# Neighbouring states of a selective scan added in pairs on GpSimd before TensorE sums them, in batch 3 of 4

## The chip, the core and the metric

The kernel runs on one core of a Trainium2 chip. The metric is the device time of one execution in microseconds (us). In the kernel before, three runs gave 2015.58, 2021.76 and 2025.78 us; their median is 2021.76 us. Engines are called PE (TensorE; PEld is its weight load), DVE (VectorE), ACT (ScalarE), POOL (GpSimd) and SP (SyncE, which here issues the DMAs).

## The reference, cut to what matters

Two layers run on x (4 batches of 512 tokens of 512 features) with a context (4 of 512 x 256): a selective state-space block gated by x, a ternary feed-forward block ("bitnet"), a cross attention with 16 heads, and four small experts. The change lies in the first block:

```python
def step(state, xs):
    d_t, B_t, C_t, u_t = xs
    dA = jnp.exp(d_t[..., None] * A)
    state = state * dA + (d_t * u_t)[..., None] * B_t[:, None, :]
    y_t = jnp.einsum('ben,bn->be', state, C_t)
    return (state, y_t)
...
y = y + D[None, :, None] * u
y = y * jax.nn.silu(z)
```

There are 512 channels, 512 steps in time and 16 states. The sum over the 16 states n in `y_t` is what the change regroups.

## The kernel before

Each batch goes through `front` (projections, L524), `scan` (L606), `bitnet` (L710) and `attention` (L826, 16 heads). Batch 0 does the first three alone. From batch 1 on, those three of batch b run beside the attention heads of batch b-1: the main loop (L1301) takes a piece of a head, then some steps of `layer0` (L1284), which is front, scan and bitnet of a later batch (`LEADS` says from which head). Batch 3's scan so runs beside the last heads of batch 1 and the first of batch 2. Below, "head 1.14" is batch 1's head 14. The order on each engine is then not that of the text: a scheduler places the instructions, and each engine works through its own list strictly in that order.

The scan takes the 512 channels as four tiles of 128 and works on two of them (t = 0, 1) at a time: a first half (t0 = 0) and a second (t0 = 2). In a half, for each state n and tile t:

- ACT makes dA = exp(delta A) in PSUM (L652);
- POOL multiplies u by B into a tile h (L656, by the helper at L186; it shows as h<-u,bc);
- DVE scans along time (L659 or L662);
- the product with C is made by DVE (L660) in six of eight steps, and by POOL (L663, by L186; it shows as h<-h,cc) in the other two, which fall on odd n and t = 1;
- PE adds the product into the accumulator `py` by four 128x128 transposes (`add`, L625, at L627), which accumulate in PSUM over all 16 states; `uds`, the D u term, is added the same way after n = 2 (L665).

B and C of each state are broadcast to all partitions by two DMAs (bc, L646; cc, L648) into tiles of tag "g", of which there are five. The tiles h have the tag "v", of which there are six (`MIDS`, L67). After a half, `silu_z` (L610) of the batch's x is used (first half) or read back (second half) for the gate, and the sum is added to x (L683). Batch 3's x takes the buffer of batch 1's x, so `load_x(3)` (L640, by L179) waits until batch 1 has left it (`finish`, L1273). `silu_z` then needs four `row_stats` (L188), whose reciprocal roots are on POOL (L183, rstz).

A head makes queries (pq) and their norms on POOL (rqs, L942), scores (ps), a softmax in two halves (L954) and the weighted sum (pav). In the heads from 9 on of batches 0 to 2, POOL makes one column of each softmax half (L984 and L986, `LO_POOL`), otherwise it makes only a scaled copy (L991). After four heads there is a projection (pwo). POOL also makes parts of the keys (rk, L874; ks, L889).

Of the kernel before, what the change touches and what calls it, by code (L numbers as in the profile page):

```python
# [35 lines left out]
ALU = mybir.AluOpType  # L36
# [10 lines left out]
DS = 16  # L47
# [44 lines left out]
SC = 4  # L92
PT = 3
MT = 0
AV = 4
VB = 2
WB = 5
# [13 lines left out]
def flamingo_kernel(  # L111
# [8 lines left out]
    nc = tc.nc  # L120
# [11 lines left out]
    def psum(pool, name, tag="m", bufs=None):  # L132
        if tag == "a":
            role = name.rstrip("_0123456789")
            if pool is psa and role in LAST_PSS and name[len(role)] == str(B - 1):
                return psum(pss, name)
            tag = ATAG.get(role, "m")
            bufs = ABUF[tag]
        kw = {} if bufs is None else {"bufs": bufs}
        return pool.tile([P, 512], F32, tag=tag, name=name, **kw)  # L140
# [12 lines left out]
    def midt(shape, dtype, name, tag):  # L153
        if tag in wider:
            pool, bufs = wider[tag]
            return pool.tile(shape, dtype, tag=f"m{tag}", name=name, bufs=bufs)
        return mid.tile(shape, dtype, tag=tag, name=name, bufs=MIDS[tag])
# [19 lines left out]
    def load_x(b):  # L177
        x_sb[b] = xpool.tile([P, T, L], F32, tag="x", name=f"x{b}", bufs=2)
        nc.sync.dma_start(x_sb[b], x[b].rearrange("(p t) f -> p t f", t=T))  # L179
# [5 lines left out]
    def pool_mult(out, a, b):  # L185
        nc.gpsimd.tensor_tensor(out, a, b, ALU.mult)  # L186

    def row_stats(xr, name, gain=1.0, res=None):  # L188

        st = sm(6, f"bst{name[0]}", f"bst{name}", 2)  # L190
        nc.vector.bn_stats(st, xr)
        mv = sm(2, f"mv{name[0]}", f"mv{name}")
        nc.vector.bn_aggr(mv, st)
        var = sm(1, f"var{name[0]}", f"var{name}")
        nc.vector.tensor_scalar(var, mv[:, 1:2], EPS, gain**-2, ALU.add, ALU.mult)
        if res is None:
            res = sm(2, f"rst{name[0]}", f"rst{name}")
        rsqrt(res[:, 0:1], var)
        nc.vector.scalar_tensor_tensor(res[:, 1:2], mv[:, 0:1], -1.0, res[:, 0:1], ALU.mult, ALU.mult)
        return res  # L200

    def normed(xr, stats, name, tag="v"):
        xn = midt([P, L], F32, f"xn{name}", tag)
        if name[0] in NRMD:
            nc.vector.tensor_scalar(xn, xr, stats[:, 0:1], stats[:, 1:2], ALU.mult, ALU.add)
        else:
            nc.scalar.activation(xn, xr, AF.Identity, bias=stats[:, 1:2], scale=stats[:, 0:1])
        return xn
# [306 lines left out]
    def transposed(pool, src, name, g=None):  # L515

        ps = psum(pool, name).rearrange("p (t e) -> p t e", t=T)
        for t, s in enumerate(src):
            nc.tensor.transpose(ps[:, t, :], s[:, g::T], ident)
        return ps[:, : len(src), :]  # L520
# [85 lines left out]
    def scan(b, of_8=DVE_OF_8, G=2, y_tile=lambda name: psum(pss, name), between=lambda n, ins: None):  # L606
        delta, du, ud_d, bd = fronts[b]
        sz_d = dram.tile([P, T, L], F32, tag="szd", name=f"szd{b}", bufs=2)

        def silu_z(t):  # L610

            xt = x_sb[b]
            w = normed(xt[:, t, :], row_stats(xt[:, t, :], f"z{b}{t}", 0.5), f"z{b}{t}")
            th = midt([P, L], F32, f"zth{b}{t}", "t")
            nc.scalar.activation(th, w, AF.Tanh)
            nc.vector.scalar_tensor_tensor(w, th, 1.0, w, ALU.add, ALU.mult)
            return w

        for t0 in range(0, T, G):
            gs = T // G
            ys = [y_tile(f"py{b}{t0}{i}").rearrange("p (g t e) -> p g t e", g=gs, t=G) for i in range(G)]

            def add(src, t, first, last):  # L625
                for g in range(T):
                    nc.tensor.matmul(  # L627
                        ys[g // gs][:, g % gs, t, :], src[:, g::T], ident, is_transpose=True,
                        start=first and t == 0 and g % gs == 0, stop=last, skip_group_check=True,
                    )  # L630

            uds, szs = [], []
            for t in range(G):
                uds.append(midt([P, L], F32, f"udr{b}{t0}{t}", "t"))
                nc.sync.dma_start(uds[t], ud_d[:, t0 + t, :])
            for n in range(DS):
                if n == 4 and x_sb[b] is None:
                    while b >= 2 and estats[b - 2] is None:
                        yield
                    load_x(b)  # L640
                if n == SZR and t0 > 0:
                    for t in range(t0, t0 + G):
                        szs.append(midt([P, L], F32, f"szr{b}{t}", "v"))
                        nc.sync.dma_start(szs[-1], sz_d[:, t, :])
                bc = midt([P, L], F32, f"bc{b}{t0}_{n}", "g")
                nc.sync.dma_start(bc, bd[n, :].partition_broadcast(P))  # L646
                cc = midt([P, L], F32, f"cc{b}{t0}_{n}", "g")
                nc.sync.dma_start(cc, bd[DS + n, :].partition_broadcast(P))  # L648
                for t in range(G):
                    nm = f"{b}{t0}{t}_{n}"  # L650
                    dA = psum(pss, f"dA{nm}")
                    last = nc.scalar.activation(  # L652
                        dA, delta[t0 + t], AF.Exp, scale=A[:, t0 + t, n : n + 1]
                    )
                    h = midt([P, L], F32, f"h{nm}", "v")
                    pool_mult(h, du[t0 + t], bc)  # L656

                    if (G * n + t) % 8 in of_8:
                        nc.vector.tensor_tensor_scan(dA, dA, h, 0.0, ALU.mult, ALU.add)  # L659
                        nc.vector.tensor_tensor(h, dA, cc, ALU.mult)  # L660
                    else:
                        nc.vector.tensor_tensor_scan(h, dA, h, 0.0, ALU.mult, ALU.add)  # L662
                        pool_mult(h, h, cc)  # L663
                    add(h, t, n == 0, n == DS - 1)
                    if n == 2:  # L665
                        add(uds[t], t, False, False)
                between(n, last.ins)
                yield

            xt = x_sb[b]  # L670
            if t0 == 0:
                szs = [silu_z(t) for t in range(T)]
                for t in range(G, T):
                    nc.sync.dma_start(sz_d[:, t, :], szs[t])
            for g in range(T):
                if g % gs == 0:
                    acc = midt([P, gs, G, P], F32, f"acc{b}{t0}{g}", "t")
                    nc.scalar.copy(acc, ys[g // gs])
                ps = transposed(pss, szs[:G], f"psz{b}{t0}{g}", g)
                a = acc[:, g % gs]  # L680
                nc.vector.tensor_tensor(a, a, ps, ALU.mult)
                xv = xt[:, g, :].rearrange("q (p e) -> q p e", e=T)[:, :, t0 : t0 + G]
                nc.vector.scalar_tensor_tensor(  # L683
                    xv, a.rearrange("q e p -> q p e"), tg[:, 0:1], xv, ALU.mult, ALU.add
                )
                yield
# [139 lines left out]
    def attention(b):  # L826
# [70 lines left out]
        def values(hg):  # L897
            def v_tile(shape, dtype, name):
                return at.tile(shape, dtype, tag="v", name=name, bufs=AV)

# [270 lines left out]
    def last_experts(pool, places):  # L1171
# [12 lines left out]
        for t in (T - 1, *range(T - 1)):  # L1184
            xTs[t] = pool.tile([P, 2, T, P], F16, tag="v", name=f"lxT{t}", bufs=AV)
            split_normed(x_sb[b][:, t, :], estats[b][t], xTs[t], slice(0, P), f"l{t}", "q")
# [22 lines left out]
    with tc.tile_pool(name="pro", bufs=1) as pro, tc.tile_pool(name="psp", bufs=4, space=PSUM) as psp:  # L1209
# [8 lines left out]

        if MT:
            wider["t"] = pro, MT  # L1220

# [14 lines left out]
        def between(n, ins):  # L1236

            if n < 0:
                for _ in range(4):
                    next(side)  # L1240
            for _ in range(2 if 0 <= n < SIDE1 else 0):
                with tc.issue_after(ins):
                    next(side, None)

        run(front(0, inp, between))
        run(scan(0, range(7), 4, iter_ps, between))
        wider.clear()
        for _ in side:
# [51 lines left out]
    n = B * NH  # L1300
    for i in range(-2, n):  # L1301
        b2, h2 = divmod(i + 2, NH)
# [112 lines left out]
```

## Time and profile before

| what | value |
|---|---|
| median of the three runs | 2021.76 us |
| the profiled execution | 2021.89 us, of which the span from first to last instruction is 2020.1 us |
| PE busy, PEld busy | 1634.6 us (81%), 899.8 us (45%) |
| DVE busy | 1541.3 us (76%) |
| ACT busy | 1333.7 us (66%) |
| POOL busy | 941.3 us (47%) |
| batch 3's scan, first half | 1092 to 1208 us |
| batch 3's x is loaded | issued at 1258.3 us |
| batch 3's scan, second half | 1273 to 1374 us |
| the last of batch 3's bitnet | 1514 us |

The page gives the busy time of each engine, and tables by stage say how much of a stretch each was busy ("x" is the number of instructions; PEclk is the granted TensorE clock as a share of full speed). A group's row has its engine, operation, tiles (result first) and shapes, then its busy time, the mean of one in ns, and the idle time of its engine ahead of it with what ended that idle time.

### The profile page before, as it was taken

How to read it: one execution, taken by the hardware profiler on the slowest of the kernel's cores; microseconds unless marked ns; L12 is line 12 of the kernel's file. 1: busy time of each engine (PE TensorE's matmuls, PEld its weight loads, DVE VectorE, ACT ScalarE, POOL GpSimd, SP SyncE). 2: the span in 40 equal slices, each digit the busy share in tenths (PEclk: the TensorE clock that was granted, in tenths of full speed). 3: DMA queues.
4: the chain of work that ended last, by engine and by line, in shares of the span. 5: the costliest groups of instructions: out<-in, count | busy, mean ns of one | idle time of the engine just before them, and what ended most of it. 6: DMA issues, size and time to landing. Idle time of an engine off the chain costs nothing. (4 is left out here: it accounts for less than half of the span.)

```text
span 2020.1 us, 27201 instructions
## 1 busy us (share of the span) xinstructions
PE 1634.6 (81%) x8366; PEld 899.8 (45%) x8366; DVE 1541.3 (76%) x2893; ACT 1333.7 (66%) x3123; POOL 941.3 (47%) x931
## 2 busy tenths in 40 slices
PE   4364698657789987778999878798999879798888
PEld 1343233344444444455444554454444445455456
DVE  5899776999998778799886984999764565654664
ACT  6787656756666876475658665666565775857673
POOL 1886311785754269385414783675133441413211
PEclk8555798767789998989999899898999889898999
DMA  7454557778775587766435887676445686767655
GB/s 269 171 166 136 161 156 229 183 223 218 219 207 130 129 216 176 210 165 164 99 87 148 192 201 190 157 183 142 96 84 131 131 212 172 205 163 181 185 138 152
DMA packets 516322, 342.50 MB, mean 170 GB/s; under 512 B 425800, under 2 KB 427976, under 8 KB 510032
## 3 DMA queue, kind: packets, MB, share of 16 engines
q1 hardware_dynamic: 516176, 340.77, 64.9%
q8 instruction: 65, 1.06, 0.2%
q14 instruction: 81, 0.66, 0.1%
HBM read 193.10 MB, written 44.30 MB: 118 GB/s over the span
## 5 line engine op out<-in xcount | busy, mean ns | idle before, releaser
L186 POOL TENSOR_TENSOR h<-u,bc 128x512 f32<-128x512 f32 x256 | 338.2, 1341 | 86.4 <-DMA bc<-bd 43.7
L627 PE MATMUL py<-ident,h 128*128 128x128 f32 x1024 | 196.4, 337 | 123.9 <-DVE h L660 95.4
L652 ACT ACTIVATE dA<-delta,A 128x512 f32<-128x512 f32 x256 | 172.4, 685 | 140.5 <-DVE h L660 105.1
L252 PE MATMUL ps<-kT,qT 128*128 128x512 f16 x768 | 213.2, 399 | 50.1 <-ACT pr L971 34.4
L252 PE MATMUL pav<-pT,v 128*128 128x256 f16 x1536 | 215.6, 296 | 42.9 <-DMA pT<-hl 19.3
L659 DVE TENSOR_TENSOR_SCAN dA<-dA,h 128x512 f32<-128x512 f32 x200 | 240.7, 1217 | 11.4 <-POOL h L186 6.6
L627 PEld LDWEIGHTS py<-ident,h 128*128 128x128 f32 x1024 | 164.3, 213 | 166.7 <-DVE h L660 122.8
L951 DVE TENSOR_REDUCE nmx<-ps 128x1 f32<-128x512 f32 x256 | 172.4, 680 | 69.1 <-PE ps L252 68.8
L252 PE MATMUL pq<-axnT,wq 128*128 128x512 f16 x768 | 206.2, 423 | 19.9 <-DVE ksq L880 7.8
L992 DVE SCALAR_TENSOR_TENSOR hl<-pr,den,hl 128x512 f16<-128x512 f32 x214 | 193.7, 923 | 32.6 <-ACT hl L989 18.3
L971 ACT ACTIVATE pr<-ps,nmx,rqs 128x512 f32<-128x512 f32 x256 | 197.7, 775 | 14.2 <-DVE hl L992 10.1
L252 PEld LDWEIGHTS <-v 128*128 128x128 f16 x1536 | 161.5, 106 | 99.6 <-issue 33.8
L252 PE MATMUL pwo<-wo,oT 128*128 128x512 f16 x768 | 178.7, 383 | 9.0 <-DVE oT L244 5.5
L991 POOL TENSOR_SCALAR hl<-pr,den 128x512 f16<-128x512 f32 x86 | 63.6, 740 | 237.9 <-issue 104.6
L252 PEld LDWEIGHTS <-wq 128*128 128x128 f16 x768 | 83.1, 109 | 130.1 <-issue 64.6
L183 POOL TENSOR_TENSOR rqs<-ssq,mhalf 128x4 f32<-128x4 f32 x64 | 68.7, 1073 | 148.7 <-ACT ssq L940 140.9
L660 DVE TENSOR_TENSOR h<-dA,cc 128x512 f32<-128x512 f32 x200 | 134.3, 679 | 4.4 <-DMA cc<-bd 0.7
L252 PEld LDWEIGHTS <-qT 128*128 128x128 f16 x768 | 76.2, 102 | 137.0 <-issue 65.2
L252 PEld LDWEIGHTS <-cT 128*128 128x128 f16 x768 | 79.0, 105 | 113.3 <-issue 45.0
L252 PEld LDWEIGHTS <-oT 128*128 128x128 f16 x768 | 74.7, 99 | 99.8 <-DVE oT L244 8.4
L989 ACT ACTIVATE hl<-pr,den 128x512 f16<-128x512 f32 x128 | 91.8, 717 | 36.4 <-DVE den L978 30.0
L252 PE MATMUL pk<-wk,cT 128*128 128x512 f16 x384 | 106.4, 420 | 11.3 <-ACT ssq L940 6.2
(387 smaller groups left out, 3481.5 us busy)
## 6 DMA issues: line engine op xcount, KB each, us to landing
bc<-bd SPq DMA_DIRECT2D x112, 256.0 KB, 4.2
cc<-bd SPq DMA_DIRECT2D x112, 256.0 KB, 3.9
wq<-dwq SPq DMA_DIRECT2D x64, 256.0 KB, 4.4
wo<-dwo SPq DMA_DIRECT2D x64, 256.0 KB, 3.5
w<-w3d SPq DMA_DIRECT2D x12, 1024.0 KB, 7.0
de<-hle SPq DMA_DIRECT2D x9, 1024.0 KB, 5.5
lw<-de SPq DMA_DIRECT2D x18, 512.0 KB, 4.9
wk<-dwk SPq DMA_DIRECT2D x16, 512.0 KB, 3.5
```

Source lines behind the costliest of these rows:

```text
L183: nc.gpsimd.tensor_tensor(res, arg, mhalf[:, : arg.shape[1]], ALU.pow)
L186: nc.gpsimd.tensor_tensor(out, a, b, ALU.mult)
L252: nc.tensor.matmul(ps, l, r, start=first and i == 0, stop=last and i == n - 1)
L627: nc.tensor.matmul(ys[g // gs][:, g % gs, t, :], src[:, g::T], ident, is_transpose=True, start=first and t == 0 and g % gs == 0, stop=last ...
L652: last = nc.scalar.activation(dA, delta[t0 + t], AF.Exp, scale=A[:, t0 + t, n : n + 1])
L659: nc.vector.tensor_tensor_scan(dA, dA, h, 0.0, ALU.mult, ALU.add)
L660: nc.vector.tensor_tensor(h, dA, cc, ALU.mult)
L951: nc.vector.tensor_reduce(nmx[:, c : c + 1], ps, AX.X, ALU.max, negate=True)
L971: mark[0] = nc.scalar.activation(pr, scs[c], AF.Exp, bias=nmx[:, one], scale=rqs[:, one], accum_out=den[:, c - c0 : c - c0 + 1],).ins
L989: nc.scalar.activation(hl[:, c, 0], prs[c], AF.Copy, scale=den[:, one])
L991: nc.gpsimd.tensor_scalar(hl[:, c, 0], prs[c], den[:, one], 1.0, ALU.mult, ALU.mult)
L992: nc.vector.scalar_tensor_tensor(hl[:, c, 1], prs[c], den[:, one], hl[:, c, 0], ALU.mult, ALU.subtract)
```

## The change

In batch 3 alone, the product of an even state is kept in its tile; when the next, odd state's product is there, POOL adds the two, and PE transposes the sum in one set of four instead of two. The D u term goes in after n = 3 instead of n = 2.

```diff
+PAIRS = (3,)
...
-            uds, szs = [], []
+            uds, szs, odd = [], [], [None] * G
...
-                    add(h, t, n == 0, n == DS - 1)
-                    if n == 2:
-                        add(uds[t], t, False, False)
+                    if b not in PAIRS:
+                        add(h, t, n == 0, n == DS - 1)
+                        if n == 2:
+                            add(uds[t], t, False, False)
+                    elif n % 2 == 0:
+                        odd[t] = h
+                    else:
+                        h2 = odd[t]
+                        nc.gpsimd.tensor_tensor(h2, h2, h, ALU.add)
+                        add(h2, t, n == 1, n == DS - 1)
+                        if n == 3:
+                            add(uds[t], t, False, False)
```

## The prediction, as put on record before the changed kernel ran

> **What bounds the kernel now.** I read the page's busy shares, then the chain that ended last, then tables by stage, then groups and waits in the stage that the change touches. The chain reaches back only into the last 70 us, where batch 3's experts are, so it says nothing of a scan that ends at 1375 us. By the page PE leads (81%), but the table by stage around batch 3's scan differs:
>
> ```profile
> 1100.00:1210.00 110.00, 89.59 (x483) 54.55 (x483) 96.55 (x132) 79.85 (x190) 86.67 (x75) 0.92 0.83 185
> 1210.00:1272.00 62.00, 50.78 (x249) 26.90 (x250) 33.94 (x81) 30.86 (x82) 21.23 (x25) 0.89 0.71 181
> 1272.00:1375.00 103.00, 85.76 (x472) 54.37 (x470) 98.72 (x137) 66.25 (x168) 71.12 (x61) 0.90 0.71 176
> 1375.00:1514.00 139.00, 130.09 (x639) 61.13 (x637) 107.87 (x262) 87.79 (x236) 47.21 (x62) 0.98 0.49 100
> ```
>
> After the stretch and its length come the busy times of PE, PEld, DVE, ACT and POOL, then the granted clock. First half of the scan: DVE 88%, PE 81%, POOL 79%. The gap between the halves: PE 82%, DVE 55%. Second half: DVE 96%, PE 83%, POOL 69%. Then bitnet and heads: PE 94%. So during the scan DVE is the fullest engine, and PE becomes the bound directly behind it.
>
> What ends the gap? VectorE's timeline shows the statistics of batch 3's x waiting for its load:
>
> ```profile
> 1263.51 1.29 DVE L191 BATCH_NORM_STATS2 bstz<-x 128x6 f32<-128x512 f32 x2 [2.88 <-DMA x<-in_x]
> ```
>
> The load was issued at 1258.3 us, after batch 1's last projection (1242 to 1252 us) and its store. On POOL the four rstz of these statistics stand ahead of the second half's first product in both builds. So the second half starts when head 1.15 is through, and not when the first half is; the first half, done at 1208 us, has over 50 us of slack.
>
> **The change part by part.** Groups of batch 3's scan, in the window 1100 to 1380 us:
>
> ```profile
> L186 POOL TENSOR_TENSOR h<-u,bc 128x512 f32<-128x512 f32 x62 | 80.2, 1307 | 17.1 <-DMA bc<-bd 8.2 <-PE py L627 5.2 <-PE psz L519 1.6
> L659 DVE TENSOR_TENSOR_SCAN dA<-dA,h 128x512 f32<-128x512 f32 x48 | 57.7, 1216 | 4.2 <-POOL h L186 3.6 <-ACT dA L652 0.5
> L627 PE MATMUL py<-ident,h 128*128 128x128 f32 x256 | 41.5, 293 | 9.0 <-DVE h L660 6.9 <-DVE den L978 1.9
> L660 DVE TENSOR_TENSOR h<-dA,cc 128x512 f32<-128x512 f32 x48 | 32.1, 676 | 1.3 <-DMA cc<-bd 0.7
> L186 POOL TENSOR_TENSOR h<-h,cc 128x512 f32<-128x512 f32 x16 | 21.3, 1328 | 17.3 <-DVE h L662 16.6 <-DVE den L978 0.7
> ```
>
> **Removed on PE:** 64 sets of four transposes become 32, so 128 transposes go (in the build, L627 has 960 instead of 1088, the D u term included). What a set costs where others queue behind it is read from PE's timeline:
>
> ```profile
> 1150.08 0.63 PE L627 MATMUL py<-ident,h 128*128 128x128 f32 x4
> 1150.55 0.81 PE L252 MATMUL ps<-kT,qT 128*128 128x512 f16 x3
> ...
> 1154.01 0.63 PE L627 MATMUL py<-ident,h 128*128 128x128 f32 x4
> 1154.48 2.75 PE L252 MATMUL pwo<-wo,oT 128*128 128x512 f16 x12
> ```
>
> The next matmul starts 0.47 us after the set, so 32 sets are 15.0 us. By busy time it is 41.5/2 = 20.7 us. Per half: 7.5 to 10.4 us.
>
> **Added on POOL:** 32 adds of 128x512 f32. The nearest rows are the 80 products of the same shape above: (80.2 + 21.3)/78 = 1.30 us. So 32 x 1.30 = 41.6 us, 20.8 per half. In the first half POOL would go from 86.7 to 107.5 us of 110, in the second from 71.1 to 91.9 of 103.
>
> **Added waits:** the add waits for the odd state's product with C. Behind it in POOL's list stand the next states' h<-u,bc (for which DVE's scan waits), the softmax pieces L984 and L986 of heads 1.11 to 1.15 (for which the DMA to pT waits), rqs (ACT's nmx) and rk (DVE's ksq). Tiles: of six "v" tiles two now stay filled while the next state is made, and the next product takes the tile that the add or the sum's transposes free; before, PE's release cost POOL 5.2 us. The latest product waiting for a tile is four steps behind instead of six. At 3.4 us a step (110/32) that is 13.7 us, against a chain of 1.3 + 1.2 + 0.7 + 1.3 + 0.5 = 5.0 us (product, scan, product with C, add, transposes). It holds unless POOL's list is late. The bc and cc DMAs stay the same in number, and in SP's list only shift with the rest; their tiles are freed as before.
>
> **Moved by the scheduler:** in DVE's list I counted the scans of batch 3 that stand ahead of a head's first reciprocal. Ahead of heads 1.12, 1.13, 1.14, 1.15: before 9, 20, 31, 32; after 8, 17, 24, 30. Ahead of heads 2.3, 2.4, 2.5, 2.6: before 42, 50, 60, 64; after 42, 47, 56, 63. On PE the bitnet's first matmul stands behind head 2.5's weighted sum before, and behind 2.7's after; its last projection stands between heads 2.9 and 2.10 in both, and behind that the lists of PE agree. So heads are pulled ahead of the scan, and by 1514 us the same work must be done.
>
> Now the sum, against the profiled 2021.9 us (the median of the runs, 2021.8, is the same):
>
> 1. *First half and gap, 1092 to 1272.* Seven steps fewer stand ahead of head 1.14: 7 x (1.22 + 0.75 x 0.68) = 12.1 us of DVE work leaves the path to the gate and goes into the gap, where DVE is idle 28 us. Best: -12. Against it 20.8 us of adds, of which POOL's 23 us of idle time take up some; these idle times are waits for others, so at worst 15 stay: +15. I take -5, nearer the gain, since the gap's POOL (21 of 62 us busy) takes part of the scan too.
> 2. *Second half, 1272 to 1375.* DVE binds, so removed PE work gives nothing here. POOL's 11 us left idle bound a loss: 0 to +10. L992 on DVE took 1.30 us in the first half (POOL 79% busy) and 0.90 in the second (69%): 16 x 0.4 = 6.4 us at most. I take +2.
> 3. *Bitnet, 1375 to 1514.* PE binds at 94%. The heads pulled ahead have left its list, and the 7.5 to 10.4 us of transposes of the second half come back here: 0 to -10. I take -6.
>
> Behind 1514 us the order is unchanged: 0. Sum -9: **2013 us**. The best by these bounds is -12 + 0 - 10, so 2000.
>
> On the contention just named, the Trainium skill (SBUF — State Buffer, section "SBUF: two separate sides") speaks against the change: GpSimd and a VectorE operation with two SBUF inputs take one port pair as an exclusive lock for a whole instruction, and the loser blocks. The rows agree in kind (L992, with pr and hl in SBUF, 0.74 to 1.77 us; L660, with dA in PSUM, always about 0.68). By the rule each of 24 L992 could wait out a whole add of 1.30 us, +31 us, and the sum would be 2044; the rows of L992 say a fifth of that.
>
> **The rivals.** *POOL becomes the bound* (slower). For: 107.5 of 110 us in the first half, and the heads that hold the gate go through the same list. The decision point is POOL above about 95% in the first half, with DVE waiting on POOL's h for over 15 us in place of 3.6. Price: half of the adds unhidden in each half, +10 and +10, less 6 in the bitnet: +14, so 2036. Against: POOL is 34% busy in the gap, and the scan now reaches into it.
>
> *Hidden, or paid back by the clock* (no change). Nothing on the path to the gate is PE's. And a thinner PE may be granted less clock: batch 0's scan, with PE 35 to 60% busy, ran at 0.50 to 0.57, these halves at 0.92 and 0.90. If it falls by 0.04, the 215 us of PE work left in 1092 to 1375 take 215 x 0.04/0.91 = 9 us more, which eats the gain: 2022. The Trainium skill (TensorE: Matmul & The Clock Gate, Part 4) says that transposes don't count as PE activity for the clock gate; by that the clock would stay, and the sum 2013; the rows can't tell these apart before the run.
>
> *It does not do what it says:* excluded, since the build has the 32 adds and 128 fewer transposes.
>
> **How the numbers follow.** Forecast 0.50 (2000 to 2022), hidden 0.20 (2016 to 2028), POOL-bound 0.30 (2026 to 2050). A measurement here can tell about 0.5%, 10 us. Below 2011.7 lies some 0.7 of the forecast: 0.36 is faster. Above 2031.9 lies most of the POOL case: 0.25 slower. The rest, 0.39, is within 0.5%. The range 1998 to 2036 reaches from the best sum, less 2 us for the spread of the runs, to the POOL case's price; the forecast's own range is 2000 to 2022.
>
> **What would show it.** Right: x of batch 3 loaded before 1258 us; POOL at 85 to 95% in the first half, and its wait groups for DVE grown by under 10 us; bitnet's last projection at 1500 to 1508 us; L627 near 22 us busy in 128 transposes. Wrong: DVE's scan waiting on POOL's h by over 15 us; the load later than 1262 us; a clock under 0.87 in either half; the time behind bitnet changed by over 5 us.

## The result, and the profile after

The change made the kernel slower by about half a per cent: its time is 1.0046 times that of the kernel before, with a 95% interval of 1.0032 to 1.0061 (22 runs of each; medians 2031.69 and 2024.61 us). By the ratio that is some 9 us; the medians alone differ by 7.1 us. The forecast was 9 us the other way. The profiled execution after took 2036.8 us, its span is 2034.8 us.

The work moved as reckoned. First the busy times on the page of the kernel after, then two of its groups, then tile h in the window 1080 to 1400 us (numbers in ns: least, median, most; then the first and last start). Line numbers are those of the changed file: those of before plus one, and plus ten behind the new block. The window closes ahead of the last step, so 30 of the 32 adds are in it.

```profile
PE 1627.7 (80%) x8238; PEld 883.1 (43%) x8238; DVE 1546.6 (76%) x2893; ACT 1333.3 (66%) x3123; POOL 982.2 (48%) x963
...
L628 PE MATMUL py<-ident,h 128*128 128x128 f32 x896 | 176.7, 343 | 119.8 <-DVE h L661 90.3
```

```profile
L673 POOL TENSOR_TENSOR h<-h,h x30: 1258/1267/1701, 1123.0 to 1394.3; 128x512 f32<-128x512 f32 x30
...
who waited for it (us, times):
  ACT dA L653: 35.3, 30
  POOL h L673: 11.5, 8
  DVE dA L660: 4.5, 6
```

128 transposes are gone (896 records for 1024; 176.7 us busy for 196.4), and POOL has 40.9 us more (982.2 for 941.3). An add takes 1.27 us in the median, as a product does. DVE's scan waited 4.5 us for POOL's h, in place of 3.6. But PE as a whole got only 6.9 us emptier, since the busy time of its other matmuls grew by 12.8 us.

Now the table by stage (columns: length; busy time of PE, PEld, DVE, ACT, POOL with the number of instructions; granted clock; the DMA engines' busy share and GB/s). Three of its stretches are those that the prediction shows of before. The first begins at 1092 us and not at 1100, so before's row for it comes first, and the four of after follow:

```profile
1092.00:1210.00 118.00, 96.03 (x521) 58.01 (x519) 102.66 (x145) 87.19 (x207) 91.57 (x80) 0.93 0.82 184
```

```profile
1092.00:1210.00 118.00, 87.49 (x451) 48.70 (x450) 94.53 (x132) 81.92 (x197) 97.94 (x86) 0.92 0.75 175
1210.00:1272.00 62.00, 46.34 (x206) 23.47 (x206) 38.34 (x67) 29.32 (x76) 30.87 (x31) 0.76 0.64 162
1272.00:1375.00 103.00, 75.38 (x384) 42.70 (x382) 89.81 (x136) 63.02 (x161) 75.12 (x65) 0.90 0.65 167
1375.00:1514.00 139.00, 126.55 (x636) 63.03 (x634) 116.48 (x260) 84.36 (x216) 63.54 (x73) 0.96 0.48 115
```

In the third stretch every engine but POOL is emptier than before: the work is late. The stretches are fixed times, so they no longer hold the same work. The gate shows the delay. The load of batch 3's x is the last start in this row of the view by line (1258.3 us before):

```profile
L180 SPq DMA_DIRECT2D x<-in_x x4: 333/384/460, 4.6 to 1273.5; - x4
```

It is 15.2 us later, and so are the last matmul of batch 3's bitnet (1524.3 us before, 1539.5 after) and the profiled time (14.9 us). Behind that nothing was lost: from the first softmax exponential of head 2.13 to the end it is 471.3 us before and 472.1 after.

### The profile page after: what moved, and what is told of

Same layout as the page of the kernel before. It is cut to its first block, busy times and chain, and to the rows that moved or that the text cites. A ratio compares the mean times of both kernels' runs of the same rounds, so it can differ in the third digit from the quotient of the medians.

```text
span 2034.8 us, 26955 instructions
## 1 busy us (share of the span) xinstructions
PE 1627.7 (80%) x8238; PEld 883.1 (43%) x8238; DVE 1546.6 (76%) x2893; ACT 1333.3 (66%) x3123; POOL 982.2 (48%) x963
## 5 line engine op out<-in xcount | busy, mean ns | idle before, releaser
L628 PE MATMUL py<-ident,h 128*128 128x128 f32 x896 | 176.7, 343 | 119.8 <-DVE h L661 90.3
L653 ACT ACTIVATE dA<-delta,A 128x512 f32<-128x512 f32 x256 | 172.8, 686 | 131.8 <-DVE h L661 105.0
L253 PE MATMUL pq<-axnT,wq 128*128 128x512 f16 x768 | 209.0, 427 | 31.4 <-DVE ksq L890 15.2
L1002 DVE SCALAR_TENSOR_TENSOR hl<-pr,den,hl 128x512 f16<-128x512 f32 x214 | 200.7, 956 | 40.2 <-ACT hl L999 25.0
L628 PEld LDWEIGHTS py<-ident,h 128*128 128x128 f32 x896 | 145.8, 213 | 160.0 <-DVE h L661 111.7
L981 ACT ACTIVATE pr<-ps,nmx,rqs 128x512 f32<-128x512 f32 x256 | 197.7, 775 | 18.8 <-DVE hl L1002 15.8
L253 PE MATMUL pwo<-wo,oT 128*128 128x512 f16 x768 | 183.5, 390 | 10.5 <-DVE oT L245 5.8
L661 DVE TENSOR_TENSOR h<-dA,cc 128x512 f32<-128x512 f32 x200 | 134.7, 680 | 3.9
L253 PEld LDWEIGHTS <-oT 128*128 128x128 f16 x768 | 75.6, 101 | 107.2 <-issue 14.9
```

The costliest lines, as they stand in the source:

```text
L253: nc.tensor.matmul(ps, l, r, start=first and i == 0, stop=last and i == n - 1)
L628: nc.tensor.matmul(ys[g // gs][:, g % gs, t, :], src[:, g::T], ident, is_transpose=True, start=first and t == 0 and g % gs == 0, stop=last ...
L653: last = nc.scalar.activation(dA, delta[t0 + t], AF.Exp, scale=A[:, t0 + t, n : n + 1])
L981: mark[0] = nc.scalar.activation(pr, scs[c], AF.Exp, bias=nmx[:, one], scale=rqs[:, one], accum_out=den[:, c - c0 : c - c0 + 1],).ins
L1002: nc.vector.scalar_tensor_tensor(hl[:, c, 1], prs[c], den[:, one], hl[:, c, 0], ALU.mult, ALU.subtract)
```

## Where the time went: lengths by heads

Two profiles of one kernel differ by some us ahead of the change, so I compare lengths between the same events: the start of the first softmax exponential (L971, after L981) of heads 1.10, 1.14, 2.1 and 2.13. The first half of the scan and the gap lie within 1.10 to 2.1, the second half and the bitnet within 2.1 to 2.13. The table holds the profiles of the study, the experiments too (they follow below), but for two: `lock` is another kernel, and `one_tile_all` has other work in the stretch (765 PE instructions from 1.10 to 2.1, where one_tile has 691; it takes 184.0 us, with PE busy for 153.8). "Steps" is the number of batch 3's scan steps that stand ahead of head 1.14 in DVE's list. "PE waits" sums the idle time of PE that the timeline ascribes to a releaser in 1.10 to 2.1, and "longest" is the longest of these waits. Each row is one execution, on one of several chips, and not always a typical one: pe_alone's was 13 us faster than its median, first_half's 10 us slower.

| kernel | ratio | steps | 1.10–1.14 | 1.14–2.1 | 1.10–2.1 | 2.1–2.13 | PE waits | longest |
|---|---|---|---|---|---|---|---|---|
| before | 1 | 31 | 109.7 | 56.5 | 166.2 | 294.9 | 29.8 | 3.3 |
| before_d9 | 1.0000 | 31 | 111.6 | 53.7 | 165.3 | 293.1 | 27.7 | 3.3 |
| d_term | 0.9973 | 31 | 108.9 | 57.8 | 166.7 | 292.8 | 33.1 | 4.6 |
| lo_before | 1.0063 | 31 | 110.1 | 58.9 | 169.0 | 303.1 | 30.4 | 4.4 |
| late_pe | 1.0063 | 32 | 109.4 | 59.6 | 169.0 | 305.5 | 33.3 | 7.4 |
| pe_alone | 0.9975 | 32 | 111.5 | 51.1 | 162.6 | 288.0 | 28.8 | 4.1 |
| second_half | 1.0005 | 31 | 110.5 | 59.2 | 169.7 | 295.0 | 32.6 | 5.1 |
| pool_alone | 1.0007 | 23 | 102.6 | 66.3 | 168.9 | 290.5 | 30.6 | 4.1 |
| add_dve | 1.0047 | 25 | 106.8 | 59.5 | 166.3 | 301.8 | 35.5 | 4.0 |
| one_tile | 0.9957 | 26 | 105.0 | 61.8 | 166.8 | 289.7 | 30.4 | 3.7 |
| one_tile_d9 | 0.9988 | 26 | 104.1 | 61.6 | 165.7 | 300.9 | 33.1 | 7.3 |
| tile0 | 0.9992 | 25 | 105.4 | 62.9 | 168.3 | 293.1 | 36.8 | 4.8 |
| lo_after | 0.9972 | 21 | 104.5 | 58.0 | 162.5 | 292.3 | 33.9 | 3.6 |
| **after** | 1.0046 | 24 | 110.1 | 70.8 | **180.9** | 293.3 | 46.0 | 6.7 |
| **again** (after, once more) | – | 24 | 110.3 | 61.5 | **171.8** | 296.1 | 43.1 | 8.1 |
| **after_d5** | 1.0083 | 24 | 109.7 | 64.3 | **174.0** | 300.2 | 43.7 | 8.7 |
| **after_d9** | 1.0020 | 24 | 109.8 | 66.0 | **175.8** | 292.5 | 41.1 | 10.4 |
| **first_half** | 1.0023 | 24 | 111.0 | 61.6 | **172.6** | 293.1 | 43.5 | 8.1 |

Three things stand in it.

1. The five profiles that hold the full change in the first half (bold) take 171.8 to 180.9 us from 1.10 to 2.1; the thirteen others take 162.5 to 169.7. The mean of the five is 8.2 us above the mean of before and its three variants without any part of the change (before_d9, d_term, lo_before: 166.8). That is about the size of the loss. But the five are three orders and not five: in this stretch PE, DVE, ACT and POOL work through the same instructions in the same order in `after`, `again` and `first_half`, and these three spread over 9.1 us. `second_half` has before's order here and takes 3.5 us more than before. Between the two groups lie 2.1 us.
2. From 2.1 to 2.13 the change gave nothing and cost nothing that can be told: 293.3 and 296.1 against 294.9. But other orders of the same work lie between 292.5 and 300.2 there (before_d9, d_term, after_d5, after_d9).
3. With 31 or 32 steps ahead of head 1.14, 1.10 to 1.14 takes 109 to 112 us. With 21 to 26 it takes 103 to 107 in six other variants (pool_alone, add_dve, one_tile, one_tile_d9, tile0, lo_after), so the steps moved back do shorten it, as forecast. They cost it again in 1.14 to 2.1. With the full change the gain is missing altogether.

The loss is idle time of PE, and not more work. From 1.10 to 2.1 PE is busy for 136.2 us on average in before and its three variants and for 131.4 in the five; it is idle for 30.5 and 43.7 us.

What PE waited for changed. PE's longest wait groups in 1090 to 1385 us before, and then after (total us, times, longest):

```profile
PE py L627 <- DVE h L660: 6.9, 8, 2.0
PE po L796 <- DMA hqT<-hq: 6.4, 3, 3.3
PE pav L252 <- DMA pT<-hl: 6.0, 4, 2.5
PE pq L252 <- DVE ksq L880: 4.0, 2, 3.2
```

```profile
PE ps L253 <- ACT pr L981: 20.9, 11, 5.8
PE pq L253 <- DVE ksq L890: 9.3, 3, 6.7
PE pav L253 <- DMA pT<-hl: 6.9, 3, 4.0
```

Before, PE's largest wait was for the scan. After, it waits for a head's own softmax (`ps`, a score product, waits until ACT has read the one before it) and for the keys (`pq` waits until DVE has made `ksq` out of the PSUM bank). One spot shows a long wait. This is the repeated run, at 1204 to 1216 us, by engine (start, duration, and in brackets the idle time before with its releaser): ACT, POOL, DVE, PE.

```profile
1204.36 0.32 ACT L882 ACTIVATE ssk<-ssk,sck 128x4 f32<-128x4 f32 x1
1205.16 0.37 ACT L950 ACTIVATE ssq<-psq,ceq,gfac 128x4 f32<-128x4 f32 x1
```

```profile
1204.16 5.39 POOL L187 TENSOR_TENSOR h<-u,bc 128x512 f32<-128x512 f32 x4
1209.52 1.01 POOL L184 TENSOR_TENSOR rk<-ssk,mhalf 128x4 f32<-128x4 f32 x1
1210.51 1.00 POOL L184 TENSOR_TENSOR rqs<-ssq,mhalf 128x4 f32<-128x4 f32 x1
```

```profile
1213.33 1.21 DVE L660 TENSOR_TENSOR_SCAN dA<-dA,h 128x512 f32<-128x512 f32 x1
1214.44 0.67 DVE L890 TENSOR_TENSOR ksq<-pk,rk 128x512 f32<-128x512 f32 x1
```

```profile
1215.17 4.50 PE L253 MATMUL pq<-axnT,wq 128*128 128x512 f16 x12 [8.13 <-DVE ksq L890]
```

The norms' inputs (ssk, ssq) are there at 1204.7 and 1205.5 us. Their roots (rk, rqs) stand in POOL's list behind four products u x B in a row, which keep them waiting for some 5 us. Between rk's end (1210.5) and ksq (1214.4) DVE works through the scans of such products (the last of them is shown). So pq, and all that stands behind it on PE, waits 8.13 us. The same four products stand directly ahead of rk in `after_d9` and `first_half`, with PE waits of 10.37 and 8.14 us for ksq. In `after_d5` they stand as two and two around one softmax column ahead of rqs, and PE waits 8.70 us for the softmax. In `after` they stand there too, but rk came later still, by 1.78 us, since its input was late (for the operation of 7.12 us below); PE's wait for ksq is 6.73 us. In the kernel before no run of four stands ahead of a root from 1085 to 1260 us (four stand in a row at 1166.7 us, ahead of a product with C), and PE's longest wait there is 3.3 us. This is read from the traces; that moving rk ahead would mend it wasn't tried.

Three things speak against it as the cause of the longer stretch. one_tile_d9 has such a run of four and a wait of 7.34 us, without the longer stretch. In pool_alone rqs and rk come as late, 4.9 and 5.7 us after their inputs, and PE, which has three sets of transposes to do meanwhile, waits at most 4.1 us. And the length is not lost there in three of the five: head 1.15 starts 130.8 us after 1.10 in the repeated run and 126.3 before, but head 2.0 starts after 148.1 us in both (first_half 148.6, after_d9 149.9; before's three variants 147.9 to 150.6). Their loss falls between 2.0 and 2.1. The rows for that piece of before, the repeated run and one_tile_d9:

```profile
1235.80:1253.80 18.00, 16.43 (x86) 8.37 (x85) 13.12 (x33) 7.22 (x19) 4.39 (x7) 1.00 0.53 142
1234.00:1257.70 23.70, 20.15 (x109) 10.72 (x109) 14.67 (x34) 7.30 (x20) 6.32 (x9) 1.00 0.70 169
1233.00:1253.40 20.40, 20.34 (x111) 10.96 (x110) 13.94 (x34) 8.34 (x23) 4.52 (x7) 1.00 0.49 122
```

PE has 109 instructions there in place of 86, so a part of its work has been put off past head 2.0, and it is idle 3.6 us in place of 1.6. one_tile_d9 has as many and is idle 0.1 us. Only `after` (155.2) and `after_d5` (154.3) are late at head 2.0 already.

One thing belongs to the profiled execution of the change alone. DVE's and POOL's timelines show one operation of 7.12 us that takes 0.72 to 1.94 us in the kernel before:

```profile
1204.82 7.12 DVE L1002 SCALAR_TENSOR_TENSOR hl<-pr,den,hl 128x512 f16<-128x512 f32 x1
```

```profile
1205.34 1.16 POOL L831 TENSOR_TENSOR xsa<-xna,xsa 128x512 f16<-128x512 f32 x1
1206.45 4.93 POOL L187 TENSOR_TENSOR h<-u,bc 128x512 f32<-128x512 f32 x4
```

It ends 0.6 us after POOL's run of four. In the repeated run the longest operation of this line is 1.79 us, and 1.10 to 2.1 is 9.1 us shorter than in the first profile. Of these 9.1 us, 6.2 are busy time of PE, whose clock there was 0.87 in the first profile and 0.91 in the repeated run, and 2.9 are idle time. The loss over 22 runs, 9 us, is less than the 14.9 us between the two profiled executions of before and after.

## The experiments

My theory was at first that the lists of POOL and PE, tied by the adds, cost the heads of the first half. The rivals were: POOL's time alone; the removed PE work being worth nothing; a conflict between DVE and POOL, which the 7.12 us suggests; and that another order alone moves the time that much. All ratios are to the kernel before; the diffs are against the changed kernel, where nothing else is said.

**first_half** and **second_half**: the change in one half alone.

```diff
-                    if b not in PAIRS:
+                    if b not in PAIRS or t0 > 0:     # first_half
+                    if b not in PAIRS or t0 == 0:    # second_half
```

> Pairs in batch 3's first half alone. Theory A (the loss lies ahead of the load of batch 3's x: POOL's adds run beside batch 1's heads 11 to 15, DVE's hl at L1002 was blocked 7.1 us by POOL, and the load moved 15 us): ratio to before 1.003 to 1.008, load of x3 issued 8 us or more later than before's 1258 us. Theory B (the loss is made in the second half, which took 108 us instead of 100): ratio 0.998 to 1.002. Theory C (only the scheduler's other order costs): no sign is forecast, but then the load is late without a blocked L1002.

> Pairs in batch 3's second half alone. Theory A: ratio 0.997 to 1.001, since the 8 us that the second half lost in the changed kernel came back in the bitnet. Theory B: ratio 1.003 to 1.006, and the second half takes 105 us or more.

Measured: 1.0023 (1.0002 to 1.0044) and 1.0005 (0.9988 to 1.0022). By its interval the first half loses; the second can't be told from no change. That agrees with the table: +6.4 us from 1.10 to 2.1 in first_half, and nothing from 2.1 on in second_half.

**pe_alone** (against before): the odd states' transposes are left out, and nothing is added, so batch 3's sum lacks the odd states.

```diff
+                    elif n % 2 == 0:
+                        add(h, t, n == 0, n == DS - 2)
```

> The 128 transposes go and no add takes their place: the products of odd states are left out of batch 3's sum. If POOL's adds are what costs: ratio 0.993 to 0.999, a gain that shows what the removed PE work is worth. If the order alone costs (theory C): ratio 1.002 or more. If the removed PE work lowers the clock: granted clock under 0.87 between 1092 and 1375 us and ratio 0.999 to 1.002.

**pool_alone** (against before): all transposes stay; POOL makes 28 adds that nobody reads.

```diff
+                    if b in PAIRS:
+                        if n % 2 == 0:
+                            odd[t] = h
+                        elif n > 2:
+                            nc.gpsimd.tensor_tensor(uds[t], odd[t], h, ALU.add)
```

> All transposes stay, and POOL makes 28 of the 32 adds into a tile that nobody reads, with the even state's tile held as long as in the change. If POOL's adds are what costs: ratio 1.004 to 1.010, at least as much as the change. If POOL's adds are hidden (theory C): 0.998 to 1.002.

Measured: 0.9975 (0.9953 to 0.9997) and 1.0007 (0.9988 to 1.0025). So leaving out 15.0 us of transposes gained some 5 us (0.6 to 9.5), which is no more than another order alone gained (d_term, below), and POOL's 28 x 1.27 = 36 us of adds cost nothing that can be told as long as nobody waits for them. The two together would give 0.9982; the change gave 1.0046. What lies between is not the two engines' work; it is the tie between them, or the order, and these two runs don't tell which.

**add_dve**: the same change with the add on DVE.

```diff
-                        nc.gpsimd.tensor_tensor(h2, h2, h, ALU.add)
+                        nc.vector.tensor_tensor(h2, h2, h, ALU.add)
```

> The pair's add moves from POOL to DVE (32 adds of about 0.68 us, 22 us of DVE in stretches where DVE is 88 and 96% busy). If POOL's list is what costs (adds late behind softmax pieces and products): ratio 0.997 to 1.002, since DVE's adds follow its own product at once. If it is the dependence as such (one set of transposes waits for two states) or the moved order: ratio 1.003 or more. By DVE's load alone up to 1.008.

Measured: 1.0047 (1.0019 to 1.0075), as slow as the change, but in its one profile elsewhere: 166.3 us from 1.10 to 2.1 (no loss), and 301.8 from 2.1 to 2.13. That DVE, the fullest engine of the second half, makes it is not shown: one_tile_d9, without adds on DVE, takes 300.9 there.

**one_tile**, **tile0**: pairs only for the second or only for the first of the two tiles.

```diff
-                    if b not in PAIRS:
+                    if b not in PAIRS or t == 0:     # one_tile
+                    if b not in PAIRS or t == 1:     # tile0 (and the sum's start on t == 1)
```

> Only the second tile (t = 1) is added in pairs, where POOL itself makes the odd state's product and the add can follow at once: 16 adds, 64 transposes fewer. If POOL's list costs by its load: half of the change, ratio 1.001 to 1.003. If the adds cost where POOL's list waits for DVE's product (t = 0 only): ratio 0.996 to 1.000.

> The mirror of one_tile: only the first tile (t = 0) is added in pairs, where DVE makes both products and POOL's add waits for DVE. If these waits in POOL's list are the cost: ratio 1.003 or more, so that this and one_tile (0.9957) add up to the change's 1.0046. If POOL's load is the cost, with a threshold that 16 adds do not reach: ratio 0.994 to 0.999, as one_tile.

Measured: 0.9957 (0.9935 to 0.9979) and 0.9992 (0.9977 to 1.0007). Half of the change does not have the loss: 166.8 and 168.3 us from 1.10 to 2.1. one_tile has the lowest ratio of all versions that make the whole sum, and its interval lies below that of the change and below 1. In it the product with C of an odd state is POOL's own (the two steps of eight), so the add waits for no other engine; in tile0 it waits for DVE.

**lo_before**, **lo_after**: before and after with POOL's softmax columns of heads 1.12 to 1.15 taken off POOL.

```diff
-LO_POOL = {(b, h, 1) for b in range(3) for h in range(9, 16)}
+LO_POOL = {(b, h, 1) for b in range(3) for h in range(9, 16) if (b, h) < (1, 12) or b == 2}
```

> The kernel before, with the softmax pieces of POOL (L984, L986) in heads 1.12 to 1.15 given to ACT and DVE. The control for lo_after. Ratio 0.997 to 1.004.

> The changed kernel with the softmax pieces of POOL (L984, L986) in heads 1.12 to 1.15 given to ACT and DVE, 8 pieces of some 2 us less on POOL in the first half. If the loss comes from POOL's list beside these heads: 0.996 to 1.002 against before, and below lo_before plus 0.2%. If it comes from the order or the dependence: 1.004 or more, as far above lo_before as the change is above before.

Measured: 1.0063 (1.0039 to 1.0088) and 0.9972 (0.9952 to 0.9993). The kernel before loses by this, the changed kernel gains 0.7%, and between these two the change makes it 0.9% faster and not 0.5% slower. 1.10 to 2.1 is 162.5 us in lo_after, the shortest of all. So the loss seems to hang on what else stands in POOL's list beside the adds. The profiles don't place it there alone: lo_after is 6.5 us shorter than lo_before from 1.10 to 2.1, but 10.8 us shorter from 2.1 to 2.13 too, where no column was moved.

**again** and **lock**: the changed kernel once more, for the 7.12 us; and a kernel of its own that puts DVE pieces with two SBUF inputs, or with one in PSUM, beside 0 to 8 POOL products in a row.

```python
for k in RUNS:          # 0, 1, 2, 4, 6, 8
    nc.scalar.activation(gate, tmp, AF.Tanh)
    for j in range(k):
        nc.gpsimd.tensor_tensor(prods[j], gate, bb, ALU.mult)
    nc.vector.tensor_tensor(tmp, ps, gate, ALU.mult)
    if kind == "two":
        nc.vector.scalar_tensor_tensor(lo, tmp, den, hi, ALU.mult, ALU.subtract)
    else:
        nc.vector.scalar_tensor_tensor(lo, ps, tmp[:, 0:1], hi, ALU.mult, ALU.subtract)
```

> The changed kernel once more, for a second profile. If the long L1002 (7.1 us, DVE's softmax piece beside six POOL instructions in a row) belongs to this order of instructions, one over 4 us stands again at head 1.14; if it was a chance of that one execution, all are under 2.1 us and the load of batch 3's x is issued under 10 us later than before.

> A kernel by itself, nothing of the reference is computed: POOL makes 0, 1, 2, 4, 6 or 8 products of 128x512 f32 in a row, and DVE beside them the softmax piece, once with both inputs in SBUF (as L992) and once with one in PSUM. If POOL in a row keeps DVE out (the Trainium skill, SBUF — State Buffer, section SBUF: two separate sides, says that the loser of the port pair blocks for a whole instruction, and leaves open what happens at the next one): the piece with two SBUF inputs grows with the number, by up to 1.25 us for each product. If DVE gets in after the running one: at most 0.75 + 1.3 us however many. With one input in PSUM: 0.7 us always.

Measured: `again` took 2026.37 us beside 2019.78 of the kernel before on the same chip (one run each); there was no long operation in it. From `lock`, DVE's timeline without and beside POOL products, then with one input in PSUM, and POOL's run of four beside each kind:

```profile
6.88 0.75 DVE L45 SCALAR_TENSOR_TENSOR los<-tmps,dens,his 128x512 f16<-128x512 f32 x1
...
31.51 1.13 DVE L45 SCALAR_TENSOR_TENSOR los<-tmps,dens,his 128x512 f16<-128x512 f32 x1
...
65.41 0.75 DVE L47 SCALAR_TENSOR_TENSOR los<-pst,tmps,his 128x512 f16<-128x512 f32 x1
```

```profile
16.17 5.37 POOL L42 TENSOR_TENSOR prod<-gate,bb 128x512 f32<-128x512 f32 x4 [0.74 <-ACT gate L40]
...
50.96 4.92 POOL L42 TENSOR_TENSOR prod<-gate,bb 128x512 f32<-128x512 f32 x4 [0.74 <-ACT gate L40]
```

DVE's piece takes 0.38 us more beside any number of products, one or eight (twice 0.44, beside a single one), and POOL's run of two or more 0.45 us more; a single product takes 1.26 us beside either kind. With one input in PSUM there is no conflict. So a conflict costs each engine some 0.4 us here, and the loser does not wait out a run of products. Only one alignment was tried: DVE's piece always started 0.6 to 0.7 us after POOL's first product; in the repeated run of the changed kernel it took up to 1.79 us. The rule of the Trainium skill (SBUF — State Buffer, section "SBUF: two separate sides") is borne out in kind. What made the single 7.12 us stays open; it isn't what the change costs on average.

**late_pe** (in place of the add and its transposes): no add; both states' transposes are issued after the odd state. It takes the lateness of PE's sets alone.

```diff
+                        add(odd[t], t, n == 1, False)
+                        add(h, t, False, n == DS - 1)
```

> No add: in batch 3 both states' sets of transposes are issued when the odd state's product is there, so the even tile is held as long as in the change and PE's work stays. If holding the tiles and the later sets cost: ratio 1.003 or more. If only POOL's adds in front of the sets do: 0.998 to 1.002.

Measured: 1.0063 (1.0040 to 1.0086), as much as the change and more. But the loss lies in 2.1 to 2.13 (305.5 us); 1.10 to 2.1 is 169.0. PE's and its weight loads' waits for DVE's h are 17.1 and 20.4 us in 1088 to 1385 us, against 6.9 and 11.2 before. One line of PE's waits:

```profile
PE py L628 <- DVE h L661: 17.1, 10, 3.9
```

So later sets make a slow version too, yet with another wait than in the change, where PE's waits for what it transposes are small (PE and PEld together 18 us before, 2 to 7 in `after`, `again`, `after_d5` and `after_d9`). Whether the lateness or the other order makes it slow, this run doesn't tell.

**d_term**, **before_d9**, **after_d5**, **after_d9**, **one_tile_d9**: the D u term is added at another state in batch 3. This changes no amount of work, only the scheduler's order, and so prices an order by itself. The change itself holds such a move, from n = 2 to n = 3. The first pair of lines is against before; one_tile_d9 has n = 9 for both tiles.

```diff
-                    if n == 2:
+                    if n == (3 if b in PAIRS else 2):    # d_term; 9 in before_d9
-                        if n == 3:
+                        if n == 5:                       # after_d5; 9 in after_d9 and one_tile_d9
```

> The kernel before with nothing but the D u term's transposes moved from n = 2 to n = 3 in batch 3. By work it costs nothing: ratio 0.999 to 1.001. What it differs from that is what a scheduler's other order alone does to the time; if that is 0.4% or more, none of the differences here can be put down to a mechanism by its size alone.

> The kernel before with the D u term after n = 9 in batch 3; d_term (n = 3) was at 0.9973. It shows how far the order alone carries the kernel before: 0.997 to 1.003.

> The changed kernel with the D u term's transposes after n = 5 instead of n = 3: the same work in another order, mostly in the second half. If the change's loss is a mechanism (adds, late sets): ratio 1.003 to 1.007, and heads 1.10 to 1.14 take 109 us or more, as in the change and in first_half. If the order alone made it: anywhere in 0.996 to 1.007.

> The same with the D u term after n = 9. Mechanism: 1.003 to 1.007 and heads 1.10 to 1.14 in 109 us or more; order: anywhere in 0.996 to 1.007.

> one_tile (0.9957) with both D u terms after n = 9. If the gain of pairs in tile 1 is a mechanism: 0.994 to 0.998. If it was the order: 0.998 or more, near before_d9.

Measured: d_term 0.9973 (0.9958 to 0.9988), before_d9 1.0000 (0.9975 to 1.0024); after_d5 1.0083 (1.0055 to 1.0111), after_d9 1.0020 (0.9994 to 1.0046); one_tile_d9 0.9988 (0.9966 to 1.0011). Under three orders the change reads 1.0046, 1.0083 and 1.0020, the kernel before 1, 0.9973 and 1.0000: even the best of the one is not under the worst of the other, and the means lie 0.6% apart. The intervals of these two overlap (0.9994 to 1.0046, and 0.9975 to 1.0024). So with POOL's list as it is the change most likely costs something; with the columns taken off POOL (lo_before, lo_after) it gains, under one order. But an order alone moves 0.3% of the kernel before and 0.6% of the changed one. In the changed kernel this spread comes from 2.1 to 2.13 (300.2 against 292.5 us), while 1.10 to 2.1 is long in both. one_tile's gain isn't settled: under the other order it can't be told from no change.

**one_tile_all**: one_tile in batches 1, 2 and 3.

```diff
-PAIRS = (3,)
+PAIRS = (1, 2, 3)
```

> one_tile in batches 1, 2 and 3, a version that could beat both kernels: if each batch gains as batch 3 did (0.43%), ratio 0.985 to 0.990; if only batch 3's place gains, 0.994 to 1.000; if POOL is too full beside batch 2's scan (96% busy between 750 and 800 us before), over 1.000.

Measured: 1.0044 (1.0028 to 1.0060). The best variant does not carry over to the other batches.

## Why the prediction was wrong

*First half and gap* (forecast -5, bounds -12 to +15): measured +8.2 by the mean of five profiles. This step failed, in two places, and I called -5 "nearer the gain". **First, the gain was read at the wrong head.** I wrote that the second half starts "when head 1.15 is through", and then counted the steps ahead of head 1.14. My own count for 1.15 was 32 before and 30 after: two steps, 2 x 1.73 = 3.5 us, leave the path to the gate and not seven. Where seven steps did leave 1.10 to 1.14 (the six variants named above: 103 to 107 us), the five or so moved ones came back in 1.14 to 2.1, which took 58 to 66 us in place of 51 to 60. DVE's 28 us of idle time in the gap did not take them for nothing. **Second, the cost was looked for in POOL's fullness, and the sum had no term for PE's waits.** POOL was at 83% in the first stretch (97.94 of 118 us), below the 85 to 95% named as harmless, and DVE's scan waited for POOL's h only 4.5 us. The load of batch 3's x was late all the same, at 1273.5 us, behind the 1262 that I had named as a sign of being wrong. What the runs show instead is PE standing idle: 43.7 us from 1.10 to 2.1 by the mean of the five, 30.5 before. I had named rqs and rk among what stands behind the add. At the spot shown, what kept them waiting was a run of products of the scan, and PE waited for what they feed. How much of the 8.2 us that is stays open.

*Second half* (forecast +2): the scans span 106 us in `after` and `again`, from 84 before. Head 2.1 to 2.6 takes 129.4 and 131.2 us for 124.6. Against this one profile of before the cost is 5 to 7 us, inside its bounds of 0 to +10 but over the value taken. L1002, named as a term, fits some 4 us of it: during these scans 16 take 17.3 and 18.4 us, where 15 took 13.7 before. But before_d9 and d_term, without any part of the change, take 133.5 and 133.3 us from 2.1 to 2.6, so the cost can't be told from that of another order.

*Bitnet* (forecast -6): from 2.6 to 2.13 the two profiles are 6.4 and 5.4 us shorter than before (163.9 and 164.9 us for 170.3). The number agrees, but it may be luck: before_d9 and d_term take 159.6 and 159.4 us there with all their transposes. The two steps together come to about nothing in place of -4. The bitnet's end that I named, 1514 us, was read from a window that closed too early: its last matmul starts at 1524.3 us before, and at 1539.5 and 1530.6 after.

*Behind the bitnet* (forecast 0): from 2.13 to the end `after` is 0.8 us longer and `again` 0.8 us shorter than before. This held, within the 5 us named.

*The prices* held: 1.27 us an add where 1.30 was taken (from 78 products, not the 80 that the text has), 176.7 us of transposes for 196.4. But a price isn't a gain: the 15 us of PE work removed gave some 5 us in pe_alone, and an order alone gave as much. In the change PE's idle time grew: from head 1.10 to 2.13 PE stood idle 64 us before and 84 in the repeated run.

*The rivals.* POOL as the bound: its sign was right, but by its own decision point it didn't happen. DVE waited for POOL's h 4.5 us and not 15, POOL stayed under 95%, and the same adds unread cost nothing. Less clock: in the fixed stretches it was 0.92 and 0.90, as before, but these no longer hold the halves. Over the scans' own spans, first and second half, before and then after:

```profile
1116.10:1205.70 89.60, 74.47 (x415) 46.98 (x414) 81.80 (x113) 59.57 (x136) 71.81 (x63) 0.93 0.87 202
1285.30:1370.60 85.30, 70.70 (x396) 45.28 (x395) 83.98 (x116) 52.38 (x126) 60.33 (x52) 0.92 0.74 177
```

```profile
1116.80:1237.30 120.50, 84.92 (x421) 46.68 (x421) 95.64 (x128) 74.05 (x186) 102.01 (x90) 0.85 0.70 173
1295.00:1402.00 107.00, 79.69 (x399) 45.73 (x398) 94.25 (x126) 63.79 (x170) 89.43 (x74) 0.87 0.64 160
```

The repeated run has 0.88 and 0.86. So the clock was 0.05 to 0.08 lower in these two profiles, and a sign that I had named, under 0.87 in either half, came true in one half of each. In the first half all five profiles of the change have 0.85 to 0.90, before and its three variants 0.89 to 0.96; in the second, after_d9 has 0.95. By the rule cited (the Trainium skill, TensorE: Matmul & The Clock Gate, Part 4) taking out transposes would by itself have left the clock as it was. Whether their absence or PE's longer waits lowered it, the runs don't tell: pe_alone has 0.88 and 0.91 without the transposes, lo_before 0.89 and 0.92 with all of them. This rival took a part. From 1.10 to 2.1 PE is busy for 134.7 and 134.4 us in the two of the five at a clock of 0.87 (`after`, `after_d9`), and for 128.6 and 128.9 us in the two at 0.91 and 0.92 (`again`, `first_half`), so it can hold up to some 6 us. It isn't the whole loss: those last two are still 5 and 6 us over the mean of before and its variants.

*What stays open.* The loss is in the first half and gap, and the stretch was long only where all of these came together: pairs in both tiles, on POOL, awaited by the sum, beside the softmax columns of heads 1.12 to 1.15; in each version without one of them it is as long as before, by one profile of one order. Late roots and a long wait of PE are seen in all five profiles. They are a reading, not an edit tried; one_tile_d9 has them without the loss, and in three of the five the length is lost only behind head 2.0. So the failed step is known, and its cause is not. All but the changed kernel have one profile, and a profile of one order doesn't tell the mechanism from the order.

## What to carry to other kernels

Follow the count to the event that opens the next stage, and read it there, not at the one before it that shows the larger number. Work taken off an engine is not gained by its price (here at best about 5 of 15 us), and adds that cost nothing unread can stand in a version that is half a per cent slower once others wait for them. Compare a stage over the span of its own work, since a fixed window hid the fall of the clock here. Before believing half a per cent in a kernel with a scheduler, run both versions under an order that differs in nothing but the place of a small neutral step.

## What the runs showed of the hardware

DVE's 128x512 piece with two SBUF inputs took 1.13 us in place of 0.75 beside POOL products, whether one or eight were in a row (it started 0.6 to 0.7 us after the first of them each time), and POOL's run of four 5.37 in place of 4.92 us; with one input in PSUM neither changed. A single execution had the same kind of piece at 7.12 us, ending 0.6 us after POOL's run of four; I found no cause for it. A POOL add of 128x512 f32 took as long as a product, 1.27 us.
